# Norm roots as one power on GpSimd, earlier key masks, the last projection and norm by halves of tokens, and a new order of work

## The chip, the cores and the metric

The kernel runs on one core of a Trainium2 chip. The metric is the time of one execution in device microseconds; lower is better. Engines are named as in the profile: PE is TensorE (PEld its weight loads), DVE VectorE, ACT ScalarE, POOL GpSimd, SP SyncE, which here only issues loads and stores.

## The reference: what is computed

Four attention layers are chained on x (4 batches of 256 tokens of width 256) with one context of the same shape, all in float32:

```
x = L0(x, ctx)   # twice: x += cross_attention(layer_norm(x), ctx), 16 heads of 128, one learned key and value;
                 # then x += gelu(layer_norm(x) @ W1) @ W2
x = L1(x, ctx)   # x += attention(layer_norm(x), ctx, key mask), 16 heads of 16; then x += MLP(layer_norm(x))
x = L2(ctx, x)   # queries from x, keys and values from ctx and x together (512), key mask;
                 # then x += MLP(rms_norm(attention + x))
x = L3(x, ctx)   # 32 query heads of 8, 8 key heads, additive mask; then layer_norm(attention + x) * gamma + beta
```

Layer norm subtracts the mean and multiplies by rsqrt(variance + eps); the RMS norm of L2 multiplies by rsqrt(mean square + eps).

## The kernel before, in words

All of x (tile X), the context's transpose (ctxT) and the weights of the layer at work stay in SBUF; 128 tokens stand on the 128 partitions, so that a batch is two token tiles. Products go through eight PSUM banks (tags pj, s, et, o), and VectorE or ScalarE copies each out.

The code writes no instructions directly. It makes a list of some 2,500 `Task`s (line 172): each has a batch, a shape on TensorE ("full" 128x128, "rows" 32 rows, "cols" 32 columns, or none), a cost, the tasks it comes after, the ring buffers it takes and gives back, and `Post`s (line 160), the work of other engines behind it with a cost for each engine that may do it. `plan` (line 1617) then walks the list in time, engine by engine, by those costs, picks at each step the task of the highest rank among those that can start soonest (rank is the longest way to the end, less a handicap by stage, batch and kind, `HANDICAPS`, line 1740), and the instructions are issued in that order. `tc.keep_in_program_order` pins it: every engine runs its queue in exactly the planned order. Line 132 (134 in the kernel after) is the helper that issues nearly everything, so the profile is read by tiles.

Stage 0 is layer 0's two attentions (over four groups of four heads, two pairs of batches), stage 1 its MLP, stages 2 and 3 attention and MLP of L1, 4 and 5 those of L2, 6 is L3 with its closing norm. From stage 1 on a batch is a unit of work, and the batches overlap.

What the change and the prediction touch:

- `norm` (line 244) makes three tasks: `stats` on VectorE (mean and variance of two token tiles, and variance + eps), `root` on ScalarE (Ln, then Exp with scale -0.5), `apply` on VectorE (one Newton step of four instructions on 128x2 values, and the scaling of both tiles). It runs 28 times: 8 in stage 0, 4 for each of the three MLPs, 4 in L1's attention, 4 in L3's `closing` (line 888).
- `Layer.fill` (line 337) runs on GpSimd when layer 0's buffers are freed: small per-layer constants, and for L1 and L2 the key mask, loaded by GpSimd with the keys on the partitions (`hraw`) and turned into `hide`.
- `attention` (line 367): its `masks` tasks load the same mask per batch along the free axis (`mraw`) and turn it into `hide_r`; `keys.plus` makes from it the term that VectorE adds to the keys. `values.fill` sets the constant columns of the value tiles.
- "rows" tasks (`scores`, `maxima`, `weights`): products over 32 rows, for two row groups each. Two tasks of different `pair` run side by side on all four row groups. `SOLO` is what the planner adds for one that runs alone.
- `ending` and `project` (lines 516 and 783): an attention's output is divided by its sums (`quotients`, tile xo), turned back, projected (tile oT, weight w3o in L3) and added to X.
- `seven` (line 1037) makes a 512-wide product from seven products of 256, with sums of weights and of context prepared by GpSimd (`sums`, `value_sums`, `differences`); its second product is added to a bank that VectorE or ScalarE must first have copied out (tile u).
- `plan`'s constants (line 1608): NEAR 0.06 and SLACK 0.2, SOLO 2.0, HELD 0.9 (how much of GpSimd's remaining work is added to some VectorE tasks).

Of the kernel before, what the change touches and what calls it, by code (L numbers as in the profile page):

```python
# [51 lines left out]
def kernel(ctx: ExitStack, tc: tile.TileContext, a: dict, out: bass.AP):  # L52
# [52 lines left out]


# [95 lines left out]
    QK, VV, EQ, OT, XO, M3, HIDES, PLUS = (Ring([]) for _ in range(8))  # L202
    PO = [Ring([None, None]) for _ in range(2)]
    SHIFTS = [Ring([]), Ring([])]
    v_holds, raws = {}, {}
# [29 lines left out]
    def plus_row_to(b, after, dst, name):  # L235


        def run(e):
            for i in range(2):
                ge.tensor_tensor(dst()[:, i, :], dst()[:, i, :], row(name), ALU.add)  # L240

        return Task(b, None, 0, None, after, posts=[Post(("POOL",), 1450, run)])

    def norm(b, after, src, eps, mean, st, take=()):


        def stats(e):
            all_ = sm.tile([P, 8], F32, tag="mv8", name="mv8", bufs=8)
            mv = st["mv"] = all_[:, 0:4].rearrange("p (i c) -> p i c", i=2)
            v = st["v"] = all_[:, 4:6]  # L250
            st["r"] = all_[:, 6:8]
# [10 lines left out]
            if mean:  # L262
                ve.tensor_scalar(v, mv[:, :, 1], eps, None, ALU.add)
            else:
                ve.tensor_scalar(v, mv[:, :, 1], 1.0 / D, eps, ALU.mult, ALU.add)

        def root(e):
            r = st["r"]
            se.activation(r, st["v"], AF.Ln)
            se.activation(r, r, AF.Exp, scale=-0.5)  # L270

        def apply(e):

            v, r, mv = st["v"], st["r"], st["mv"]
            h = sm.tile([P, 2], F32, tag="ih", name="ih", bufs=2)
            ve.tensor_tensor(h, v, r, ALU.mult)
            ve.tensor_tensor(h, h, r, ALU.mult)
            ve.tensor_scalar(h, h, -0.5, 1.5, ALU.mult, ALU.add)
            ve.tensor_tensor(r, r, h, ALU.mult)
            st["apply"](mv, r)  # L280
# [10 lines left out]
        t = Task(b, None, 0, None, after, takes=take, posts=[Post(("DVE",), 1150, stats, near=True)])  # L291
        t = Task(b, None, 0, None, [t], posts=[Post(("ACT",), 400, root, EXP)])
        return Task(b, None, 0, None, [t], posts=[Post(("DVE",), 1400, apply, near=True)])
# [32 lines left out]
    class Layer:  # L326
# [9 lines left out]

        def fill(self):
# [15 lines left out]
            if key != 3:  # L353
                for g in range(2):
                    ge.tensor_scalar(
                        self.bkx[:, :, g], bk, sel16[:, g : g + 1], rowof[:, SHIFT[g] : SHIFT[g] + 1],
                        ALU.mult, ALU.add,
                    )

                mask, dtype = self.given  # L360
                raw = late_tile([P, B * S // P], f"hraw{key}", dtype=dtype)
                with nc.allow_non_contiguous_dma(reason="a mask, once"):
                    ge.dma_start(raw, mask.rearrange("o (c p) -> p (o c)", p=P))
                self.hide = late_tile([P, B * S // P], f"hide{key}")
                ge.tensor_scalar(self.hide, raw, 0.0, HIDE, ALU.is_equal, ALU.mult)

    def attention(L, b, after, hTs, dst, dst_after, weights_at):
# [11 lines left out]
        if key == 3:  # L379
# [3 lines left out]
            masks = Task(b, None, 0, None, after, takes=[(M3, st, "m")], posts=[Post(("SP",), 100, fetch)], lag=4.0)  # L383
        else:
            def fetch(e):
                ge.dma_start(raws[key], L.given[0][:, b * S : (b + 1) * S].to_broadcast([P, S]))

            def hidden(e):
                ge.tensor_scalar(st["hide_r"][2], raws[key], 0.0, HIDE, ALU.is_equal, ALU.mult)

            t = Task(b, None, 0, None, after, takes=[(HIDES, st, "hide_r")], posts=[Post(("POOL",), 700, fetch)], lag=3.0)
            masks = Task(b, None, 0, None, [t], posts=[Post(("POOL",), 1000, hidden)])
# [19 lines left out]
        def keys(t, after, q, give):  # L412
# [16 lines left out]
            for g in range(2):  # L429
# [6 lines left out]
                def add(e, g=g):  # L436
# [5 lines left out]
                    Task(b, None, 0, None, [masks], takes=[(PLUS, pl, g)], posts=[Post(("POOL",), 560, plus)])  # L442
# [14 lines left out]
        def values(si, after, give):  # L457
# [28 lines left out]
            t = Task(b, None, 0, None, after, takes=[(VV, st, f"V{si}")], posts=[Post(("POOL",), 600, fill)])  # L486
# [17 lines left out]
        for t in range(2):  # L504
            tq = queries(t, after, qs[t])
# [3 lines left out]
        if key != 3:  # L509
            Task(b, None, 0, None, behind=with_mask, gives=[(HIDES, st, "hide_r")])  # L510
        vs = [values(si, after, []) for si in range(len(L.sources))]
# [58 lines left out]
        def unit8(t, q):  # L570
            u = {}
            S_tasks, V_tasks = [], []
            for j in range(4):
                turned, Ss = [], []
                grab = Task(
                    b, None, 0, None, S_tasks or ready[t] + [masks],
                    takes=[(EE, u, j)] + ([(PO[1], u, "pm"), (PS, u, "po")] if j == 0 else []),
                )
                for pair in range(2):
# [30 lines left out]
                    for i in range(2):  # L610
# [5 lines left out]
                        def turns(i=i, v=v):  # L616
                            for kc in range(2):
# [10 lines left out]
                                b, "full", 0.47, turns, [tx], takes=[(PS, v, ("t", i))],  # L628
# [32 lines left out]
        def unit16(t, q):  # L661
# [55 lines left out]
            for kc in range(NCK):  # L717
                Ws = []
                grab = Task(
                    b, None, 0, None, shifted,  # L720
# [60 lines left out]
        w = {}  # L781

# [105 lines left out]
    def closing(b, after):  # L888
        st = {"xn": None}

        def apply(mv, r):
            for i in range(2):
                y = Xb(b)[:, i, :]
                ve.scalar_tensor_tensor(y, y, mv[:, i, 0:1], row("L3_xattn_gamma"), ALU.subtract, ALU.mult)
                ve.scalar_tensor_tensor(y, y, r[:, i : i + 1], row("L3_xattn_beta"), ALU.mult, ALU.add)
                dma.dma_start(out_t[:, b, i, :], y)

        st["apply"] = apply
        norm(b, after, lambda: Xb(b), 1e-6, True, st)
# [14 lines left out]
    for g in range(4):  # L914
        nc.gpsimd.dma_start(
            rows[_CS_ROWS:, :].rearrange("t (k g d) -> t k g d", k=4, g=4)[:, :, g, :], bk3
        )

# [36 lines left out]
    def columns(i, after, lag):  # L955
# [20 lines left out]
        return t if i == 2 else Task(0, None, 0, None, [t], posts=[Post(("POOL",), 800, scaled)])  # L976
# [25 lines left out]
    def differences(b, after, block, T):  # L1002
# [10 lines left out]
        return Task(b, None, 0, None, after, posts=[Post(("DVE", "POOL"), {"DVE": 1320, "POOL": 2900}, run, near=True)])  # L1013
# [9 lines left out]
    def sums(b, after, behind, w, key):  # L1023
# [11 lines left out]
        return Task(b, None, 0, None, after, posts=[Post(("POOL",), 2900, run)], behind=behind)  # L1035
# [102 lines left out]
    def context_sums(b):  # L1138
# [12 lines left out]
        return Task(b, None, 0, None, [t_ctx[b]], posts=[Post(("DVE", "POOL"), {"DVE": 840, "POOL": 1600}, run, near=True)])  # L1151
# [3 lines left out]
    def value_sums(after, behind, w):  # L1155
# [12 lines left out]
        return Task(0, None, 0, None, after, posts=[Post(("POOL",), 2900, run)], behind=behind)  # L1168
# [4 lines left out]
    for li in range(2):  # L1173
# [35 lines left out]
        for hg in range(NG):  # L1209
# [31 lines left out]
            def run(e, w=w):  # L1241
# [4 lines left out]
                0, None, 0, None, [t_bv], posts=[Post(("DVE", "POOL"), {"DVE": 600, "POOL": 1270}, run, near=True)]  # L1246
            )
            of_w = []
            for bp in range(2):
# [12 lines left out]
                t_learned = Task(b0, None, 0, None, [grab, t_cols[li]], posts=[Post(("POOL",), 400, learned)])  # L1262
# [224 lines left out]
    def run(e):  # L1487
# [15 lines left out]
        (XO, 1, [P, 2, P], "xo"),  # L1503
        (M3, 2, [P, 2, S], "m3"),
        (HIDES, 1, [P, S], "hide_r"),
# [3 lines left out]
    def open_late(e):  # L1509
# [12 lines left out]
        raws[1] = late_tile([P, S], "mraw1", mybir.dt.uint8)  # L1522
        raws[2] = late_tile([P, S], "mraw2", mybir.dt.int32)
# [15 lines left out]
    opened.fills = [(r, len(r.tiles), len(r.tiles) + n) for r, n, _, _ in later] + [(r, 0, 2) for r in SHIFTS]  # L1539
# [10 lines left out]
    def run(e):  # L1550
# [9 lines left out]
        k: Task(0, None, 0, None, [opened, t_rows], posts=[Post(("POOL",), 3500, lambda e, k=k: layers[k].fill())], lag=2.0)  # L1560
# [13 lines left out]
    for b in range(B):  # L1574
# [8 lines left out]
        at1 = attention(layers[1], b, [tt, t_w1, t_L[1]], st, lambda b=b: (Xb(b), Xb(b)), [tp], [])  # L1583
# [7 lines left out]
            [(EE, s2, "fT")],  # L1591
# [8 lines left out]
        to = attention(layers[3], b, [tt, t_w3, t_L[3]], st, lambda b=b: (Xb(b), Xb(b)), [tp], [])  # L1600
        closing(b, [to])
# [6 lines left out]
    LATE, NEAR, SOLO, TABLE, SLACK, HELD = 0.2, 0.06, 2.0, 1.3, 0.2, 0.9  # L1608
# [8 lines left out]
    def plan(handicap):  # L1617

        clock = {"PE": 0.0, "DVE": 3.3, "ACT": 2.0, "POOL": 5.5, "SP": 3.8}
# [4 lines left out]
        by_batch, by_kind = handicap  # L1626
# [18 lines left out]
        def do(group, start):  # L1645
# [16 lines left out]
            for t, p in queue:  # L1662
                def ends(e):
# [4 lines left out]
                    return begin + more + p.ns[e]  # L1668
# [176 lines left out]
```

## Time and profile before

| | us |
|---|---|
| median of 3 runs (lowest, highest) | 1366.13 (1364.66, 1367.18) |
| the profiled execution | 1366.06 |
| its span, first to last instruction | 1364.3 |
| mean granted TensorE clock | 0.991 |
| busy: PE, DVE, ACT, POOL | 1314.1, 831.3, 705.0, 190.3 |

The profile's page gives busy times by engine, forty slices of the span with one digit of busy tenths each, the chain of work that ended last, and the costliest groups of instructions. A line of a timeline gives the start, the length and the engine of one run of equal instructions, out tile<-in tiles, shapes and count, and in brackets how long the engine was idle before it and what ended that. A line of the table of stretches gives the stretch, its length, the busy time of PE, PEld, DVE, ACT and POOL in it, the granted TensorE clock, the DMA share and GB/s. A float32 matmul leaves two records, a turn (transpose by the identity) one.

### The profile page before, as it was taken

What the parts mean: (1) busy time and instruction counts of PE and PEld (TensorE: products, weight loads), DVE (VectorE), ACT (ScalarE), POOL (GpSimd) and SP (SyncE); (2) the same over time, 40 slices, a digit from 0 to 9 for tenths busy, and PEclk for the clock granted to TensorE, in tenths of its full rate; (3) what the DMA queues carried; (4) which work ended last, traced back from release to release, by engine and by line L of the source; (5) the groups of instructions that cost most, each with busy time, mean ns of one, the idle gap of its engine ahead of it and who ended that gap; (6) DMA issues with size and microseconds to landing.
All of it is one profiled execution on the core that took longest, in us unless ns stands there. A gap on an engine that the chain in (4) does not pass through costs nothing. (4 is left out here: it accounts for less than half of the span.)

```text
span 1364.3 us, 22474 instructions
## 1 busy us (share of the span) xinstructions
PE 1314.1 (96%) x8523; PEld 1038.3 (76%) x8523; DVE 831.3 (61%) x2305; ACT 705.0 (52%) x1717; POOL 190.3 (14%) x324
## 2 busy tenths in 40 slices
PE   7899999999999999999999899999999999999996
PEld 4788878888888788788888776677666668767764
DVE  7738546465664764755563468655567442886795
ACT  3445345345353453445544345644463554898795
POOL 7402020001321200200001422011011001000000
PEclk9999999999999999999999999999999999999998
DMA  6010020200200102001011320000000000000000
GB/s 230 17 47 1 1 78 1 77 1 1 78 17 31 31 1 78 1 0 47 1 67 53 92 79 4 5 1 5 6 1 5 2 1 1 1 13 13 2 10 16
DMA packets 25628, 38.01 MB, mean 28 GB/s; under 512 B 2244, under 2 KB 16086, under 8 KB 25392
## 3 DMA queue, kind: packets, MB, share of 16 engines
q1 hardware_dynamic: 24640, 35.56, 7.8%
q0 software_dynamic: 608, 0.76, 0.5%
q8 instruction: 67, 1.10, 0.4%
q14 instruction: 41, 0.34, 0.1%
q10 hardware_dynamic: 272, 0.26, 0.1%
HBM read 35.52 MB, written 1.05 MB: 27 GB/s over the span
## 5 line engine op out<-in xcount | busy, mean ns | idle before, releaser
L132 ACT ACTIVATE eq<-eq,nm 128x256 f32<-128x256 f32 x256 | 106.1, 503 | 0.5 <-DVE nm L132 0.5
L132 POOL TENSOR_TENSOR X<-X,rowbc 128x256 f32<-128x256 f32 x56 | 41.5, 762 | 410.9 <-DVE e L132 144.6
L132 DVE TENSOR_SCALAR E<-E,rinv 128x257 f32<-128x257 f32 x256 | 91.0, 420 | 2.3
L132 PE MATMUL ps_et<-qk 32*128 32x256 f32 (+1 forms) x254 | 79.9, 480 | 0.8 <-DVE shift L132 0.8
L132 PE MATMUL ps_s<-qk 32*128 32x256 f32 (+1 forms) x274 | 74.0, 464 | 5.8 <-DVE qk L132 5.5
L132 PE MATMUL ps_o<-qk 32*128 32x256 f32 (+1 forms) x266 | 73.7, 462 | 0.3 <-DVE eq L132 0.3
L132 PE MATMUL ps_pj<-qk 32*128 32x256 f32 (+1 forms) x230 | 64.5, 456 | 0.0
L132 POOL COPY kT<-lks 128x4 f32<-128x4 f32 x32 | 5.8, 195 | 378.6 <-PE ps_s L132 168.9
L132 PE MATMUL ps_et<-eq,qk 32*128 32x256 f32 x212 | 48.9, 402 | 0.2 <-DVE shift L132 0.2
L132 PE MATMUL ps_s<-eq,qk 32*128 32x256 f32 x204 | 48.8, 402 | 0.0
L132 PE MATMUL ps_pj<-eq,qk 32*128 32x256 f32 x184 | 47.0, 403 | 0.3 <-DVE shift L132 0.3
L132 DVE TENSOR_REDUCE shift<-ps_et 128x1 f32<-128x512 f32 (+1 forms) x58 | 39.3, 685 | 11.0 <-PE ps_pj L132 4.7
L132 PEld LDWEIGHTS ps_s<-qk 32*128 32x128 f32 x274 | 35.3, 187 | 12.2 <-issue 8.8
L132 DVE TENSOR_TENSOR X<-ps_et,X 128x512 f32<-128x512 f32 (+1 forms) x16 | 10.5, 658 | 55.4 <-PE ps_et L132 55.4
L132 ACT ACTIVATE E<-ps_o,nm 128x257 f32<-128x257 f32 x63 | 30.0, 477 | 27.6 <-DVE nm L132 27.4
L132 ACT ACTIVATE E<-ps_pj,nm 128x257 f32<-128x257 f32 x66 | 31.2, 476 | 22.2 <-DVE nm L132 22.1
L132 PE MATMUL ps_o<-eq,qk 32*128 32x256 f32 x168 | 42.5, 402 | 0.0
L132 PEld LDWEIGHTS ps_et<-qk 32*128 32x128 f32 x254 | 36.1, 188 | 8.2 <-issue 3.0
L132 PE MATMUL ps_et<-wo,cT 128*128 128x256 f32 x176 | 39.6, 379 | 0.0
L132 PEld LDWEIGHTS ps_o<-qk 32*128 32x128 f32 x266 | 35.1, 188 | 5.9 <-issue 2.9
L132 PE MATMUL ps_et<-kT,qT 128*128 128x257 f32 x122 | 34.9, 385 | 4.6 <-POOL X L132 4.5
L132 PE MATMUL ps_s<-kT,qT 128*128 128x257 f32 x132 | 39.1, 382 | 0.0
(581 smaller groups left out, 3868.6 us busy)
## 6 DMA issues: line engine op xcount, KB each, us to landing
wk<-in_L_xattn_wk_dram SPq DMA_DIRECT2D x8, 512.0 KB, 5.8
wv<-in_L_xattn_wv_dram SPq DMA_DIRECT2D x8, 512.0 KB, 6.8
wq<-in_L_xattn_wq_dram SPq DMA_DIRECT2D x8, 512.0 KB, 7.7
wo<-in_L_xattn_wo_dram SPq DMA_DIRECT2D x8, 512.0 KB, 4.0
bvb<-in_bv_dram SPq DMA_DIRECT2D x8, 256.0 KB, 7.8
bvl<-in_cols_dram SPq DMA_DIRECT2D x8, 256.0 KB, 7.8
f<-in_L_xattn_w_fc_dram SPq DMA_DIRECT2D x2, 1024.0 KB, 5.7
f<-in_L_xattn_mlp_w_dram SPq DMA_DIRECT2D x2, 1024.0 KB, 5.3
```

Of the source, the lines that this page charges most:

```text
L132: return lambda *args, **more: tc.keep_in_program_order(f(*args, **more))
```

## The change

The root becomes two instructions on GpSimd: add eps, raise to -0.5 (`minus_half` is a constant tile). The Newton step goes. The masks `hraw` are loaded by GpSimd at the start, behind its first loads; `fill` only tests them. The `masks` tasks of the attentions come after the work before the norm (`before`) and not after the transposed input, and there are two `hide_r` tiles, into which L2's row mask is loaded directly. L3's projection is cut into a first part (the first 128 of the reduction, both token tiles) and two parts of the second 128, one for each token tile, each followed by its own addition and its own closing norm. There are two xo tiles. Several planner costs are new (mostly higher, GpSimd's above all), three constants of `plan` and a factor on all VectorE and ScalarE costs ("wide") are now the last entry of `HANDICAPS`, HELD is 1.0, and the table of handicaps is another one, so nearly all instructions stand in a new order.

```diff
+    minus_half = const.tile([P, 2], F32, tag="mh", name="mh")
+    nc.vector.memset(minus_half, -0.5)
...
-            if mean:
-                ve.tensor_scalar(v, mv[:, :, 1], eps, None, ALU.add)
-            else:
-                ve.tensor_scalar(v, mv[:, :, 1], 1.0 / D, eps, ALU.mult, ALU.add)
-
-        def root(e):
-            r = st["r"]
-            se.activation(r, st["v"], AF.Ln)
-            se.activation(r, r, AF.Exp, scale=-0.5)
+        def root(e):
+            v, r, var = st["v"], st["r"], st["mv"][:, :, 1]
+            if mean:
+                ge.tensor_scalar(v, var, eps, None, ALU.add)
+                ge.tensor_tensor(r, v, minus_half, ALU.pow)
+            else:
+                ge.tensor_scalar(v, var, 1.0 / D, eps, ALU.mult, ALU.add)
+                ge.tensor_tensor(r, v, minus_half, ALU.pow)
...
-            v, r, mv = st["v"], st["r"], st["mv"]
-            h = sm.tile([P, 2], F32, tag="ih", name="ih", bufs=2)
-            ve.tensor_tensor(h, v, r, ALU.mult)
-            ve.tensor_tensor(h, h, r, ALU.mult)
-            ve.tensor_scalar(h, h, -0.5, 1.5, ALU.mult, ALU.add)
-            ve.tensor_tensor(r, r, h, ALU.mult)
-            st["apply"](mv, r)
+            st["apply"](st["mv"], st["r"])
...
+        def load(self):
+            mask, dtype = self.given
+            self.raw = const.tile([P, B * S // P], dtype, tag=f"hraw{self.key}", name=f"hraw{self.key}")
+            with nc.allow_non_contiguous_dma(reason="a mask, once"):
+                nc.gpsimd.dma_start(self.raw, mask.rearrange("o (c p) -> p (o c)", p=P))
...
-                raw = late_tile([P, B * S // P], f"hraw{key}", dtype=dtype)
-                with nc.allow_non_contiguous_dma(reason="a mask, once"):
-                    ge.dma_start(raw, mask.rearrange("o (c p) -> p (o c)", p=P))
                 self.hide = late_tile([P, B * S // P], f"hide{key}")
-                ge.tensor_scalar(self.hide, raw, 0.0, HIDE, ALU.is_equal, ALU.mult)
+                ge.tensor_scalar(self.hide, self.raw, 0.0, HIDE, ALU.is_equal, ALU.mult)
...
-            t = Task(b, None, 0, None, after, takes=[(HIDES, st, "hide_r")], posts=[Post(("POOL",), 700, fetch)], lag=3.0)
-            masks = Task(b, None, 0, None, [t], posts=[Post(("POOL",), 1000, hidden)])
+            t = Task(
+                b, None, 0, None, before, takes=[(HIDES, st, "hide_r")] + raw, posts=[Post(("POOL",), 700, fetch)], lag=3.0
+            )
+            masks = Task(b, None, 0, None, [t], posts=[Post(("POOL",), 1150, hidden)], gives=raw)
...
+            def part(k, qts):
+                for qt in qts:
+                    pe(
+                        w["pt"][2][:, qt * D : (qt + 1) * D], st["oT"][2][:, k, qt * P : (qt + 1) * P], L.w[3][:, k, :],
+                        k == 0 and qt == 0, k == 1, skip_group_check=True,
+                    )
+
+            def half(e, qt):
+                base, to = dst()
+                ve.tensor_tensor(to[:, qt, :], w["pt"][2][:, qt * D : (qt + 1) * D], base[:, qt, :], ALU.add)
+
+            first = Task(
+                b, "full", 0.86, lambda: part(0, (0, 1)), ends[:1] + dst_after, takes=[(PS, w, "pt")]
+            )
+            parts = []
+            for qt in range(2):
+                parts.append(
+                    Task(
+                        b, "full", 0.43, lambda qt=qt: part(1, (qt,)), [first, ends[1]], behind=list(parts),
+                        posts=[Post(("DVE",), 340, lambda e, qt=qt: half(e, qt), gives=[(PS, w, "pt")] if qt else [])],
+                        gives=[(OT, st, "oT")] if qt else [],
+                    )
+                )
+            return parts
...
+    for k in (1, 2):
+        layers[k].load()
...
-        (XO, 1, [P, 2, P], "xo"),
+        (XO, 2, [P, 2, P], "xo"),
         (M3, 2, [P, 2, S], "m3"),
-        (HIDES, 1, [P, S], "hide_r"),
+        (HIDES, 2, [P, S], "hide_r"),
...
-    LATE, NEAR, SOLO, TABLE, SLACK, HELD = 0.2, 0.06, 2.0, 1.3, 0.2, 0.9
+    LATE, TABLE, HELD = 0.2, 1.3, 1.0
...
-                    return begin + more + p.ns[e]
+                    return begin + more + p.ns[e] * wide
...
+        (0.4, 0.24, 0.71, 1.08),
```

The last line holds near, slack, solo and wide. The closing norm (not shown) is the same three steps for one token tile at a time, with its store.

## The prediction

> **What bounds the kernel now.** I read the page first (busy shares, slices, chain), then the table of stretches, then the waits of TensorE alone by stretch, then the timelines of the stretches where it waits. The page gives the bound:
>
> ```profile
> PE 1314.1 (96%) x8523; PEld 1038.3 (76%) x8523; DVE 831.3 (61%) x2305; ACT 705.0 (52%) x1717; POOL 190.3 (14%) x324
> ...
> POOL 7402020001321200200001422011011001000000
> ```
>
> TensorE is busy for 1314.1 of 1364.3 us, so work taken off another engine pays only where TensorE waits for it: 50.2 us in all. GpSimd stands at 14%, but its slices say where it is full: at the opening (7, 4) and around slice 23. The table of stretches (stretch, length, then busy time by engine) splits the 50.2:
>
> ```profile
> 0.00:50.00 50.00, 37.23 (x123) 23.64 (x124) 37.13 (x89) 16.11 (x41) 32.97 (x59) 0.93 0.47 158
> 50.00:700.00 650.00, 638.58 (x3152) 553.52 (x3151) 386.45 (x903) 300.31 (x853) 77.15 (x128) 0.99 0.09 30
> 700.00:800.00 100.00, 94.41 (x512) 81.38 (x511) 45.40 (x129) 38.68 (x87) 21.68 (x52) 0.98 0.21 63
> 800.00:1300.00 500.00, 493.23 (x4249) 346.02 (x4248) 313.75 (x972) 303.81 (x628) 58.51 (x87) 1.00 0.03 7
> 1300.00:1364.30 64.30, 50.62 (x495) 33.77 (x492) 48.54 (x214) 46.08 (x111) 0.00 (x0) 0.94 0.04 14
> ```
>
> TensorE idles 12.8 us in the opening, 11.4 in layer 0, 5.6 at the change of layers, 6.8 in layers 1 to 3, 13.7 at the end. The single waits that make these up, from the waits and the timelines (start, length, then idle time and its releaser in brackets):
>
> ```profile
> 39.05 1.20 PE L132 MATMUL ps_et<-kT,qT 128*128 128x257 f32 x2 [4.54 <-POOL X L132]
> ```
> ```profile
> 202.01 1.54 PE L132 MATMUL ps_o<-HT,f 128*128 128x256 f32 x4 [3.01 <-DVE u L132]
> ```
> ```profile
> 756.09 0.26 POOL L132 TENSOR_SCALAR hide<-hraw 128x8 f32<-128x8 uint8 x1 [7.83 <-DMA hraw<-in_mask_dram]
> ...
> 763.49 0.26 POOL L132 TENSOR_SCALAR hide<-hraw 128x8 f32<-128x8 int32 x1 [4.33 <-DMA hraw<-in_mask_dram]
> ```
> ```profile
> 776.35 0.80 PE L132 MATMUL ps_s<-qk 32*128 32x256 f32 x2 [5.49 <-DVE qk L132]
> ```
>
> At 39.05 the X sum of GpSimd is only the latest event. VectorE is the cause: it hasn't been idle since 7.0 us and finishes the qT that this matmul reads at 38.91. At 202.01 (and 556.79, alike) VectorE is late too: its four quotients on E take 3.2 us since GpSimd runs sums beside them (0.82 us each beside GpSimd's sums, 0.35 alone, from the single records). At 756 and 763 GpSimd stands still for two mask loads; what is queued behind them (row sums 766.64 to 770.8, the row mask's load, its fill, the key terms to 777.4) makes TensorE wait at 776.35.
>
> **The change, part by part.** The sum is made against the profiled execution's 1366.06 us (span 1364.3 and 1.8 around it), which lies within the three runs (1364.66 to 1367.18, median 1366.13).
>
> Counted from the two orders of instructions: TensorE has 4953 matmuls and turns in both. VectorE goes from 2307 to 2173 instructions: 28 times five small ones go (0.19 for the epsilon, 0.19, 0.16, 0.21, 0.18 for the Newton step, 0.93 us a norm, 26 us in all). ScalarE loses 56 roots of 0.20 and 4 of 18 table loads of 1.28, 16 us. GpSimd gains 64 small ones (an epsilon and a power for each of 24 norms and 8 half norms). None of it is TensorE's own time, so only the stretches count.
>
> *Opening: -5.0 (ends 0 and -6.9).* In front of the qT at 38.9, VectorE's order loses four epsilons (0.17, 0.17, 0.17, 0.40), four Newton steps (1.78, 1.72, 0.78 and 1.67, stretched by GpSimd's sums), the second bvb difference (0.60, now GpSimd's) and the fourth batch's two normalised tiles (1.43, now behind it): 8.9 us from an engine that was never free. TensorE can win what it idles behind VectorE: 4.54 at 39.05 and 2.3 at three waits for xn (17.75, 20.10, 20.90); the rest (4.64 and 1.2) are first loads that nothing changes. Against it: the roots now stand in GpSimd's queue, the first behind four sums of 0.73 that start when ctxT is there (7.4), so not before 10.4; VectorE's first statistics end about then (7.4 + 0.2 + 1.6 + 1.2). The two mask loads cost GpSimd 1.0 each at 5.7, where it was idle for 1.84; 0.2 shows. Their 5 KB join loads at a DMA share of 0.93, behind wk and x, ahead of nothing that TensorE asks for before 23. I take -5.0, nearer the far end since VectorE's sum is larger than the gap.
>
> *The power itself.* No row shows one. Below stands the 128x16 difference (0.23), above the 256-wide mask test (1.08). With its epsilon (0.2 to 0.3) a root is 0.5 to 1.4; it replaces 0.44 on ScalarE and 0.75 on VectorE with one hop fewer. I take 0.6, near the small row, and count the middle of the program at nothing.
>
> *Layer 0: -8 (ends 0 and -14).* The order is new, so I asked what makes a wait: a task placed too near behind the one that it waits for. Walking both orders at 0.43 us a 128x256 matmul and 0.1 to 0.2 a change of tile shape, and taking off the copies between at 0.3 to 0.6, 166 of layer 0's 744 TensorE tasks had under 1 us to spare before and 73 have now; with less than nothing, 23 and 1. The idle time is 11.4, and each wait costs more than its idle time: the turns at 198.07 would have been followed at 198.5, the next matmul came at 202.01, 3.5 for 3.01. So some 14 are there, and 56% of the tight places go: -8.
>
> *Change of layers: -5.0 (ends -3 and -5.5).* The two waits (7.83, 4.33) and issues (1.01, 0.97) leave GpSimd's order here, 14.1 us. In the new order the row masks no longer wait for the layer's transposed input. 5.49 goes; 0.5 is kept for three norm roots (0.6 each) that now stand in this queue ahead of the key terms. SP's order puts layer 2's four weights ahead of the MLP's two (1 MB more, landing 12.0 after their issue at worst now); the MLP asks for them some 20 us later, so nothing.
>
> *Layers 1 to 3: -1 (ends +4 and -5).* By the same walk 72 tight tasks become 62: 14% of 6.8.
>
> *Row-group pairs: +7.0 (ends +3.5 and +7.0).* The order before runs the score products of 32 rows always as two tasks side by side on the four row groups, 128 times. The new one has 120 pairs and 16 tasks alone (planned with the price of a lone one cut from 2.0 to 0.71). A pair takes 0.87 because its records in one row group follow each other at 0.21 (1293.52, 1293.74, 1293.95); a lone task has the same four. So 8 x 0.87 more, unless the second half fills time that was idle anyway.
>
> *Changes of shape: -1.4.* 311 become 298, at 0.11 (a first record 0.32 before the next, not 0.21).
>
> *End: -2.2 (ends -1.2 and -3.9).* From 1352.75, where the last turns end, to the end are 11.55: projection 3.40, add 0.75, statistics 1.4, roots 0.5, Newton 0.75, scale and shift 1.85, the store's 2.9. By halves: the first token half is projected at 0.43 x 6 = 2.55, its add and statistics end at 3.7, its root at 4.5; the second half's root at 5.3, its scale and shift, behind the first half's, at 6.4, the store's 2.9: 9.3. The projection's eight records stand 0.43 apart here, twice the 0.21 of elsewhere, at a granted clock of 0.50 (stretch 1354 to 1356.2); I keep 0.43, since the waits for the quotients ahead of them stay, and at 0.21 they would save 1.7 more, the far end. The Trainium skill (TensorE: Matmul & The Clock Gate, "Part 1: The HAM clock gate") says that TensorE falls to half clock after an idle window of about 3.4 us and needs as long a busy one to return; the trace agrees with the half, though the waits ahead of it here are of 0.6 to 1.2 each. By that rule the sum stays as it is; were a busy stretch enough to keep the clock, it would be 1349.
>
> Sum: -5.0 - 8 - 5.0 - 1 + 7.0 - 1.4 - 2.2 = -15.6, so 1350.5, put as **1350**.
>
> **The rivals.**
> *Waits go nearly everywhere (0.16).* All far ends: -6.9 - 14 - 5.5 - 5 + 7 - 1.4 - 3.9 = -29.7, 1336. For it: one tight place below zero in layer 0. Against: VectorE and ScalarE are full as well from 1290 on (9.96 of 10 us for ScalarE at 1330 to 1340).
> *Waits only move (0.17).* Spare time by count is not the late queue itself. Then layer 0 and layers 1 to 3 give nothing, the opening 3, the rest as above: -3 - 5 + 7 - 1.4 - 2.2 = -4.6, 1361.
> *GpSimd's queue becomes the norm's wait: slower (0.14).* Each root stands in order behind sums of four (2.9 us) or a mask load (up to 3.0 between issue and test). If half of the 32 roots show 2.0 each to TensorE, 32 us come on top: 1382. It decides from 15.6 / 32 = 0.5 us shown a root. For it: seven roots stand right behind such groups. Against: GpSimd's share is 14%, and batches are interleaved, so TensorE has other work.
> *A power's code is fetched at its first use (0.03).* GpSimd's first sum (0.45) and first scalar (0.31) were no longer than the next, and the longest unexplained gap is 0.4; so by rows 1351. The Trainium skill (GPSIMD Engine Reference, "2.1 Instruction dispatch") gives some 6 us for the first call of a freshly loaded kernel; in the opening that would make about 1356 by its figure.
> That the change does not do what it says is excluded by the order: 32 powers on GpSimd, no Newton step left.
>
> **How the numbers follow.** 0.50 for the forecast (1342 to 1358). A measurement here can tell about 0.2%, 2.7 us, so "same" is 1363.4 to 1368.8. Faster: 0.50 + 0.16 + 0.03 + 0.12 of "only move" = 0.81; same 0.06; slower 0.13. The range 1334 to 1364 reaches both neighbours and leaves out the slow rival and the edges.
>
> **What would show it.** Opening: first kT,qT matmul before 36. Layer 0 (50 to 700): TensorE idle under 6, no wait of 3.0 on u. Layers' change: no wait on hraw, first qk products with no idle over 1. Lone tasks: TensorE's busy time some 7 longer in layers 1 to 3. End: 9 to 10 us behind the last turns. Wrong if TensorE waits for tiles behind a GpSimd root, or if new waits of over 2 us stand in layer 0.

## The result, and the profile after

The changed kernel takes **1351.53 us** (median of 4, 1349.59 to 1353.99), beside 1365.93 us of the kernel before on the same chip (4 runs): a ratio of 0.9896, 95% interval 0.9876 to 0.9915. That is 14 us less; the prediction was 1350. Run again later it gave 1351.24 us, ratio 0.9890 (0.9877 to 0.9904). The profiled execution is the one of 1349.59 us (span 1347.8), 16.5 less than the profiled one before.

The page after, engine shares and GpSimd's slices:

```profile
PE 1313.6 (97%) x8523; PEld 1050.7 (78%) x8523; DVE 813.5 (60%) x2171; ACT 691.3 (51%) x1659; POOL 218.4 (16%) x385
...
POOL 9420010200142002000015231030010020110000
```

TensorE is busy for the same time as before (1314.1); what went is idle time, 50.2 to 34.2 us. The table of stretches after (stretch, length, busy by engine, granted clock, DMA share, GB/s) says where:

```profile
0.00:50.00 50.00, 42.75 (x174) 30.51 (x175) 39.06 (x96) 22.20 (x62) 45.14 (x77) 1.00 0.51 167
50.00:700.00 650.00, 646.86 (x3239) 567.05 (x3238) 393.18 (x895) 299.54 (x842) 76.99 (x131) 1.00 0.09 29
700.00:800.00 100.00, 97.71 (x623) 80.78 (x622) 43.57 (x107) 35.13 (x69) 38.32 (x80) 1.00 0.24 77
800.00:1300.00 500.00, 487.38 (x4117) 346.16 (x4116) 303.00 (x924) 298.66 (x603) 54.74 (x90) 0.99 0.02 4
1300.00:1347.80 47.80, 38.88 (x379) 26.21 (x376) 34.72 (x152) 35.80 (x84) 3.18 (x8) 0.95 0.04 13
```

TensorE's idle time, before and after: opening 12.8 and 7.3, layer 0 11.4 and 3.1, change of layers 5.6 and 2.3, layers 1 to 3 6.8 and 12.6, end 13.7 and 8.9. Four stretches gave time back and one took some. (From 700 on the same stretch doesn't hold quite the same work in both: from 800 to the last turns, where the work ends alike, the idle time is 12.3 and 14.7.)

The single waits after, as the timelines have them. The opening: the first kT,qT product stands at 28.66 (before 39.05), with one short wait ahead of it.

```profile
27.73 1.10 PE L134 MATMUL ps_pj<-craw,f 128*128 128x256 f32 x4 [0.72 <-DVE u L134]
...
28.66 0.60 PE L134 MATMUL ps_s<-kT,qT 128*128 128x257 f32 x2
```

The change of layers: no wait on hraw is left, but a root stands behind the fills in GpSimd's queue. Its statistics were done at 712.49; the root starts at 718.30, VectorE waits 4.70 for it, and TensorE 2.29 for VectorE.

```profile
712.31 0.18 DVE L134 BATCH_NORM_AGGREGATE mv<-st 128x2 f32<-128x6 f32 x1
...
717.11 1.10 POOL L134 TENSOR_SCALAR bqx<-cols,selq 128x2 f32<-128x2 f32 x4
718.30 0.22 POOL L134 TENSOR_SCALAR mv<-mv 128x2 f32<-128x2 f32 x1
718.61 0.72 POOL L134 TENSOR_TENSOR mv<-mv,mh 128x2 f32<-128x2 f32 x1
...
719.36 0.73 DVE L134 TENSOR_SCALAR e<-X,mv 128x256 f32<-128x256 f32 x2 [4.70 <-POOL mv L134]
...
719.88 0.82 PE L134 MATMUL ps_et<-ident,e 128*128 128x128 f32 x4 [2.29 <-issue]
```

TensorE's row says only "issue": it is the e of VectorE, one step up the chain, that is late. Layer 3's projection by halves has a wait that the prediction did not foresee, here at 1191.53, and alike at 1250.65 (2.62):

```profile
1188.21 0.70 PE L134 MATMUL ps_pj<-w3o,oT 128*128 128x256 f32 x2
...
1191.06 0.42 DVE L134 TENSOR_TENSOR X<-ps_pj,X 128x256 f32<-128x256 f32 x1
...
1191.53 0.70 PE L134 MATMUL ps_pj<-w3o,oT 128*128 128x256 f32 x2 [2.62 <-DVE X L134]
```

The first two records of TensorE are the first half of the tokens, the next two the second half. Both halves lie in one PSUM bank, and the second waits until VectorE has added the first to X. That add takes 0.42 of the wait; for most of the rest VectorE works off eight instructions on another tile (eq, 0.42 each, from 1188.30) that stand ahead of the add in its queue. The end shows it too, with 0.52:

```profile
1338.82 1.46 PE L134 MATMUL ps_o<-w3o,oT 128*128 128x256 f32 x6
...
1340.32 0.42 DVE L134 TENSOR_TENSOR X<-ps_o,X 128x256 f32<-128x256 f32 x1 [1.72 <-PE ps_o L134]
...
1340.79 0.70 PE L134 MATMUL ps_o<-w3o,oT 128*128 128x256 f32 x2 [0.52 <-DVE X L134]
1341.53 0.42 DVE L134 TENSOR_TENSOR X<-ps_o,X 128x256 f32<-128x256 f32 x1 [0.79 <-PE ps_o L134]
```

The halves follow each other instead of overlapping. But the projection's records stand 0.22 apart here, not 0.43: the clock held.

### The profile page after: what moved, and what is told of

Read it like the earlier page. It is cut to its first block, busy times and chain, and to the rows that moved or that the text cites. A ratio compares the mean times of both kernels' runs of the same rounds, so it can differ in the third digit from the quotient of the medians.

```text
span 1347.8 us, 22397 instructions
## 1 busy us (share of the span) xinstructions
PE 1313.6 (97%) x8523; PEld 1050.7 (78%) x8523; DVE 813.5 (60%) x2171; ACT 691.3 (51%) x1659; POOL 218.4 (16%) x385
## 4 chain that ended last, share of the span: by engine, by line
PE 90%; DVE 7%; ACT 2%; issue 1%; DMA 1%; POOL 0%; SPq 0%; DVEq 0%; ACTq 0%
PE ps_o L134 23%; PE ps_pj L134 23%; PE ps_s L134 23%; PE ps_et L134 21%; DVE E L134 2%; DVE eq L134 1%; ACT eq L134 1%; DVE shift L134 1%; DMA wk<-in_L_xattn_wk_dram 1%; ACT qk L134 0%; DVE qk L134 0%; DVE X L134 0%; DVE e L134 0%; DVE craw L134 0%; DVE xo L134 0%
## 5 line engine op out<-in xcount | busy, mean ns | idle before, releaser
L134 DVE TENSOR_SCALAR E<-E,rinv 128x257 f32<-128x257 f32 x256 | 97.9, 445 | 2.3
L134 PE MATMUL ps_s<-qk 32*128 32x256 f32 (+1 forms) x270 | 85.2, 476 | 0.0
L134 POOL TENSOR_SCALAR mv<-mv 128x2 f32<-128x2 f32 (+1 forms) x32 | 7.4, 233 | 454.9 <-DVE mv L134 454.4
L134 PE MATMUL ps_pj<-qk 32*128 32x256 f32 (+1 forms) x242 | 75.2, 470 | 0.0
L134 PE MATMUL ps_pj<-eq,qk 32*128 32x256 f32 x224 | 55.2, 405 | 0.0
L134 DVE TENSOR_REDUCE shift<-ps_s 128x1 f32<-128x512 f32 (+1 forms) x54 | 36.5, 683 | 20.9 <-PE ps_o L134 11.3
L134 POOL TENSOR_SCALAR plus<-hide_r,rowof,bkx 128x256 f32<-128x256 f32 x32 | 17.7, 559 | 146.6 <-DVE qk L134 146.2
L134 DVE TENSOR_TENSOR X<-ps_o,X 128x256 f32<-128x256 f32 (+1 forms) x20 | 10.4, 518 | 51.2 <-PE ps_o L134 51.2
L134 DVE TENSOR_TENSOR X<-ps_pj,X 128x512 f32<-128x512 f32 (+1 forms) x18 | 10.3, 573 | 50.1 <-PE ps_pj L134 50.1
L134 DVE TENSOR_REDUCE shift<-ps_o 128x1 f32<-128x512 f32 (+1 forms) x47 | 31.8, 683 | 13.6 <-PE ps_et L134 5.4
```

What stands on the lines that cost most here:

```text
L134: return lambda *args, **more: tc.keep_in_program_order(f(*args, **more))
```

## The experiments

Each was timed in five rounds against the kernel before on the same chip. Unless said otherwise each keeps the planner's order and changes only what is issued.

**The change's parts alone, in the order of before.** `before_masks` issues the two mask loads with the opening's:

```
-                    ge.dma_start(raw, mask.rearrange("o (c p) -> p (o c)", p=P))
...
+    for k in (1, 2):
+        layers[k].load()
```

> The kernel before with one edit: the two mask loads (hraw) are issued with the opening's loads, the order of all else kept. The theory of the prediction (the two GpSimd waits of 7.83 and 4.33 us at 756 and 763 are what delays the key terms, and so the first qk products): 1361 us, 3 to 5.5 less than before, and the 5.49 us wait of TensorE at 776 is gone. Rival (the products wait for something else that is nearly as late, the key terms' own chain or the row mask): 0 to 1 us less, a wait of 4 or more stays at the same matmul.

Measured 1361.78 us (before 1366.15), ratio 0.9963 (0.9951 to 0.9976): 4.4 less, and the wait of 5.49 at the first qk products is 0.51:

```profile
772.69 0.48 PE L132 MATMUL ps_s<-qk 32*128 32x256 f32 x2 [0.51 <-DVE qk L132]
```

The theory holds. `before_roots` moves epsilon and root to GpSimd, and takes Newton's step out, in the place of the old root:

```
-                ve.tensor_scalar(v, mv[:, :, 1], eps, None, ALU.add)
+                ge.tensor_scalar(v, var, eps, None, ALU.add)
...
-            se.activation(r, st["v"], AF.Ln)
-            se.activation(r, r, AF.Exp, scale=-0.5)
+            ge.tensor_tensor(r, v, minus_half, ALU.pow)
...
```

> The kernel before with one edit: epsilon and root as two GpSimd instructions in the place where ScalarE's Ln and Exp stood in the order, Newton's step and epsilon gone from VectorE; the order of all else kept, table loads kept. The theory of the prediction (what the lighter VectorE gives is the opening's queue behind qT, and the middle gives nothing): 1361 to 1363 us, about 3 to 5 less, all of it before 50 us and at the end. Rival 1 (VectorE's 26 us less empty its queue everywhere): about 1355, with the waits on u at 202 and 557 shorter. Rival 2 (in an order that did not plan for it, roots stand behind GpSimd's sums and mask loads): 1370 or more, with TensorE waiting for tiles behind a GpSimd root.

Measured 1361.33 us (1356.55 to 1364.22), ratio 0.9959 (0.9944 to 0.9974): 4.8 less. The theory's total came out, but as the sum of a larger gain and a loss that rival 2 had named. The stretches of this kernel (in its slowest execution, 1364.22, which is the profiled one):

```profile
0.00:50.00 50.00, 43.09 (x164) 29.91 (x165) 35.20 (x85) 18.51 (x48) 42.67 (x75) 1.00 0.49 168
700.00:800.00 100.00, 87.40 (x463) 74.22 (x462) 37.57 (x93) 32.39 (x68) 25.94 (x61) 0.93 0.21 60
```

The opening idles 6.9 instead of 12.8, at a clock of 1.00 instead of 0.93; this edit alone makes the whole gain of the change's opening. The change of layers idles 12.6 instead of 5.6, since two roots stand behind the mask loads and the work queued behind these (GpSimd's order and TensorE's wait, from the timeline):

```profile
748.31 0.26 POOL L135 TENSOR_SCALAR hide<-hraw 128x8 f32<-128x8 uint8 x1 [8.09 <-DMA hraw<-in_mask_dram]
...
760.47 0.72 POOL L135 TENSOR_TENSOR mv<-mv,mh 128x2 f32<-128x2 f32 x1
...
761.86 1.08 PE L135 MATMUL ps_et<-ident,eq 128*128 128x128 f32 x4 [12.05 <-issue]
```

`before_both` has both edits.

> The kernel before with both edits, masks early and roots on GpSimd, order kept. If the parts add up as the theory has it: about 1357, 9 less than before, and the other 5 of the change's 14 belong to the new order (with its halves and rings). Rival (the new order gives nothing of its own, the gain is the two edits): about 1352. Rival (each edit's gain needs the new order): 1363 or more.

Measured 1357.39 us, ratio 0.9939 (0.9925 to 0.9953): 8.8 less, nearly the sum of the two (9.2); the wait of 12.05 is 6.29, now behind the copy of Wk, which waits for its load. The other 5.6 of the change's 14.4 are what the rest of the change does in sum (order, halves, tiles), for and against.

**Layer 0's waits: amount or order?** `before_quotients_later` moves one task in VectorE's queue, at two places:

```
+    for at in (376, 1050):
+        steps.insert(at + 4, steps.pop(at))
```

> The kernel before with one edit of the order: in layer 0 the second group of four quotients on VectorE (3.1 us beside GpSimd's sums) is moved behind the two row minima, u and the q sum that stood behind it, at the two places whose TensorE waits on u are 3.01 us each (202.01 and 556.79); TensorE's, ScalarE's and GpSimd's orders are unchanged, and no work is taken away. Theory (layer 0's waits come from the place of a task in VectorE's queue, not from how much VectorE has to do, so an order alone takes them away, as the new order did): both waits go, 5 to 6 us less than before, about 1360.5. Rival (VectorE is simply late there, and the quotients come to be what TensorE waits for): no less than 1 us is gained, and a wait on E or eT of some 3 us stands in the place of each.

Measured 1360.71 us (before 1366.58), ratio 0.9960 (0.9947 to 0.9974): 5.9 less with no work removed. At the first place (before: 3.01 on u at 202.01):

```profile
200.25 0.55 PE L132 MATMUL ps_pj<-ident,E 128*128 128x128 f32 x3 [1.71 <-DVE E L132]
200.63 1.03 PE L132 MATMUL ps_o<-HT,f 128*128 128x256 f32 x4
```

The waits on u are gone; a wait of 1.7 on E stands in the place of each, where the rival said 3. So 1.3 of idle time is saved at each. The rest of the 5.9 is the clock's: behind the waits of 3.01 TensorE was granted 0.57 from 202 to 206, and 0.69 and 0.88 from 556 to 564, which by its busy time loses 1.7 and 1.5; behind those of 1.7 it was granted 1.00. So the order alone is worth this much, with the same amount of work. It does not take all of the wait: the 1.7 that stays at each place is a wait for the quotients, which is what the rival said, at about half its size.

**What a lone row-group task costs.** `after_lanes_alone` issues the two tasks of every pair one after the other:

```
-            while lanes:
-                for lane in list(lanes):
-                    if next(lane, lane) is lane:
-                        lanes.remove(lane)
+            for lane in lanes:
+                for _ in lane:
+                    pass
```

> The changed kernel with one edit: in every one of its 120 pairs of row-group tasks the products of the two tasks are issued one task after the other, and not in turn; same products, same order of all else. Theory of the prediction (a task alone takes as long as a pair, 0.87 us, since its four records follow each other at 0.21): about 0.87 us more for each pair, 104 in all if TensorE's time is what counts there, 1440 to 1455. Rival (the two tasks' records overlap across row groups even when they are issued one after the other, or a task alone costs TensorE only half of a pair): 1351 to 1375, and then the price of 7 us for the 16 lone tasks of the change was too high.

Measured 1351.01 us, ratio 0.9888 (0.9874 to 0.9901): no difference from 1351.24, and none of the theory's 104 us. The order of issue inside a pair costs nothing: in this trace a pair issued so still takes 1.08 (860.75 to 861.83), since the records of its two tasks overlap anyway. It says nothing on a task with other work behind it, so the conclusion that I had written beside the rival was too wide. `before_pairs_apart` settles that: at 24 places the next full-array task is issued between the two of a pair.

```
...
+            for _ in group[0].run():
+                pass
+            between[0].run()
+            for _ in group[1].run():
+                pass
...
```

> The kernel before with one edit of TensorE's order: at 24 places where a pair of row-group tasks stands ahead of a full-array task that needs neither of them, that full task is issued between the two, so that each of the two runs alone; same work, and the orders of VectorE, ScalarE and GpSimd are unchanged. Theory of the prediction (a task alone costs as much as a pair, 0.87 us, and each place adds two changes of shape of 0.11): 18 to 27 us more than before, 1384 to 1393. Rival (a task alone costs half of a pair): 3 to 8 us more, 1369 to 1374.

Measured 1399.29 us, ratio 1.0250 (1.0233 to 1.0267): 33 more, 1.37 a place, above the theory's range. From this kernel's timeline, two lone tasks with their eight records each:

```profile
804.41 1.13 PE L132 MATMUL ps_s<-eq,qk 32*128 32x256 f32 x8
805.48 0.66 PE L132 MATMUL ps_et<-ident,eq 128*128 128x128 f32 x4
806.06 1.13 PE L132 MATMUL ps_pj<-eq,qk 32*128 32x256 f32 x8
807.12 1.07 PE L132 MATMUL ps_et<-e,V 128*32 128x256 f32 x16
```

From start to next start a lone task holds TensorE for 1.06 to 1.07; a pair, 16 records, for 1.08. Summed from the trace (start to next start, idle time taken off), the 32-row products hold TensorE for 149.5 us in the kernel before, 173.5 in this one, 162.2 in the changed kernel, with the same records in all three. So these products cost 12.7 more in the changed kernel; part of that is half clock (below).

**The wait on X.** `after_parts_ahead` issues both halves of the second k part ahead of both adds:

```
-                        b, "full", 0.43, lambda qt=qt: part(1, (qt,)), [first, ends[1]], behind=list(parts),
+                        b, "full", 0.43, lambda qt=qt: None if qt else part(1, (0, 1)), [first, ends[1]], behind=list(parts),
```

> The changed kernel with one edit in the order kept: in layer 3's projection the second half of the second k part is issued with the first half, ahead of both adds (the later task emits nothing), so that no matmul writes to the bank while VectorE's add of the first half reads it. Theory (TensorE's four waits for X, 2.62 at 1191, 2.62 at 1251, 0.63 and 0.52 at the end, are made by the split, since the two halves share a bank): 4 to 6 us less than the changed kernel, about 1346, no wait on X at ps_pj, ps_et and ps_o in layer 3. Rival (VectorE is late there anyway, and the matmuls behind wait for its next results instead): within 1.5 us of the changed kernel.

Measured 1342.77 us, ratio 0.9826 (0.9811 to 0.9842); the changed kernel's control is `after_again`, 1351.24.

> The changed kernel unchanged, as the control for the others of this call: 1350 to 1353 us, as in its first runs (median 1351.5).

The waits on X are gone; the projection runs on with both halves, and the two adds follow later:

```profile
1189.88 1.13 PE L134 MATMUL ps_pj<-w3o,oT 128*128 128x256 f32 x4
...
1192.72 0.75 DVE L134 TENSOR_TENSOR X<-ps_pj,X 128x256 f32<-128x256 f32 x2
```

The gain is 8.5 by the medians, above the 4 to 6 expected and above the 6.4 that the four waits add up to. The clock is the likely rest: its mean is 0.995 over the four executions of this kernel and 0.992 over the eight of the changed kernel, some 3 us. How it comes about, the two profiled executions of the changed kernel show. In the first, behind the wait of 2.62 (stretches of 2 us):

```profile
1192.00:1194.00 2.00, 2.00 (x11) 1.75 (x10) 0.42 (x1) 2.00 (x7) 0.00 (x0) 1.00 0.00 0
1194.00:1196.00 2.00, 2.00 (x13) 1.76 (x12) 0.18 (x1) 0.80 (x2) 0.00 (x0) 1.00 0.00 0
```

In `after_again`, behind the same wait of the same length:

```profile
1192.00:1194.00 2.00, 2.00 (x5) 1.64 (x6) 0.42 (x1) 2.00 (x6) 0.00 (x0) 0.50 0.00 0
1194.00:1196.00 2.00, 2.00 (x6) 1.55 (x6) 0.00 (x0) 1.11 (x3) 0.00 (x0) 0.50 0.00 0
```

The granted clock falls to half in one and not in the other (the eighth number of a line), for 6.8 us, some 3 us lost on top. Behind the second such wait it is the other way round: the clock falls for 3.4 us behind 1250.65 in the first and holds behind 1253.94 in `after_again`. So a wait of this length costs between 2.6 and 5.6. Over all of TensorE's records the half clock takes 6.8 us in the first execution and 9.8 in `after_again`, which is most of the 3.3 by which their spans differ. The Trainium skill (PSUM — Partial Sum Buffer, "Terms") says that TensorE and another engine must not touch the same bank and quadrant at once; the trace agrees in that the second half, which writes other columns of the bank, waits for the reader of the first. That wait is for a semaphore of the program, so no run here shows what the chip would do without it.

**The root in GpSimd's queue.** `after_fills_later` emits the fills of layers 2 and 3 with Wk's head-wise copy:

```
+        layers[2].fill()
+        layers[3].fill()
         w3 = layers[3].w
...
+        k: Task(0, None, 0, None, [opened, t_rows], posts=[Post(("POOL",), 2100, lambda e, k=k: layers[k].fill() if k == 1 else None)])
```

> The changed kernel with one edit: GpSimd's fills of layers 2 and 3 (selq, bqx, bkx, hide, 3.5 us), which stand ahead of a norm's root at 718.3 in its queue, are emitted with the head-wise copy of Wk instead, some 6 us later; TensorE's order is kept. Theory (TensorE's 2.29 us at 719.88 is a wait for a tile whose root stands in GpSimd's queue from 712.5 to 718.3): 2 to 2.3 us less than the changed kernel, the wait at ps_et<-ident,e gone. Rival (the fills' new place delays the key terms by as much, or VectorE's other work holds the tile): within 1 us of the changed kernel.

Measured 1348.26 us, ratio 0.9868 (0.9855 to 0.9882): 3.0 less than the control, more than the 2 to 2.3 expected. The wait was the queue; the same turns now stand without one:

```profile
718.55 0.60 PE L134 MATMUL ps_et<-ident,e 128*128 128x128 f32 x4
```

`after_two_powers` doubles every power:

```
                 ge.tensor_tensor(r, v, minus_half, ALU.pow)
+                ge.tensor_tensor(r, v, minus_half, ALU.pow)
...
```

> The changed kernel with every power issued twice (the second writes the same root again), which puts 0.72 us (0.57 for the half norms) more behind each of the 32 statistics, 22 us more on GpSimd. Theory (a root on GpSimd is hidden beside other batches' work in most places, and shown in the opening, at 719.88 and at the end only): 1 to 3 us more than the changed kernel, 1352.5 to 1354.5. Rival (the root stands on TensorE's way wherever a norm is): 8 us or more on top, 1360 or more.

Measured 1356.82 us, ratio 0.9926 (0.9914 to 0.9939): 5.6 more than the control, between the theory's 1 to 3 and the rival's 8. Of some 22 us more on GpSimd a quarter shows, 0.17 a root: mostly hidden, but less well than I thought. The wait at 719.88 has grown from 2.29 to 3.05; where the rest shows isn't settled, since waits that lower the clock differ between single executions.

**Together.** `after_ahead_fills` has both of the mended places.

> The changed kernel with both edits of the earlier runs, the second k part of layer 3's projection ahead of both adds and the fills of layers 2 and 3 behind the norms' roots. If the two gains (8.8 and 3.0 by their medians against the changed kernel) are separate, as theirs are different waits in different stages: 1339 to 1342 us, faster than both kernels. Rival (what waits behind one comes to be shown by the other): 1343 or more.

Measured 1340.21 us (1336.51 to 1342.76), ratio 0.9802 (0.9785 to 0.9819): 11.0 less than the control, the two gains nearly added. It beats both kernels.

One thing was left: in all seven profiles of the new order up to here the clock falls for 7 to 10 us from about 810 on, with no wait over 0.5 us ahead of it. The stretches of this kernel there:

```profile
806.00:810.00 4.00, 3.35 (x17) 2.11 (x19) 4.00 (x9) 0.00 (x0) 0.77 (x2) 0.95 0.00 0
810.00:814.00 4.00, 4.00 (x23) 2.67 (x23) 3.98 (x9) 1.02 (x2) 2.08 (x3) 0.50 0.12 24
814.00:818.00 4.00, 4.00 (x34) 3.44 (x30) 2.65 (x4) 1.27 (x2) 2.19 (x3) 0.50 0.06 13
```

TensorE is recorded as busy for 3.35 of the first 4 us and all the time behind them, but much of it with lone row-group tasks, which use half of the array's rows. `after_full_between` adds full-array products there, whose result is overwritten:

```
+        if group[0].shape == "rows" and len(group) == 1 and (group[0].stage, group[0].b) == (2, 1) and "maxima" in group[0].kind:
+            bank_ = next(h[k][2] for r, h, k, i in taken if r is PS)
+            for _ in range(2):
+                pe(bank_[:, :S], ident, rowbc[:, :S], True, True)
```

> The kernel of the last combination (parts ahead, fills later) with idle work added: two 128x256 products on the full array (0.43 us each at full clock), whose result is overwritten, ahead of each of the four lone maxima tasks of batch 1 in layer 1 (around 807 to 816), 3.4 us in all. In every run of the new order so far TensorE's granted clock falls to 0.5 from 810 to some 820, with no wait over 0.5 us ahead of it, in this stretch of lone row-group tasks. Theory (row-group tasks that fill half of the array or less count to the clock as idling does): with full-array work between them the granted clock stays at or near 1.00 in 806 to 824, and the time is 1 to 3 us less than the 1340.2 of the combination in spite of the added work. Rival (the clock falls there for another reason): the clock is 0.5 in that stretch as before, and the time is 3 to 7 us more.

Measured 1338.56 us (1338.04 to 1340.2; before 1366.73), ratio 0.9796 (0.9782 to 0.9809). The same stretches:

```profile
806.00:810.00 4.00, 4.00 (x28) 2.76 (x24) 4.00 (x8) 0.00 (x0) 0.50 (x2) 1.00 0.00 0
810.00:814.00 4.00, 3.74 (x32) 2.31 (x30) 3.57 (x9) 1.13 (x3) 1.96 (x3) 1.00 0.18 30
814.00:818.00 4.00, 3.86 (x33) 2.66 (x32) 2.84 (x5) 1.86 (x4) 2.19 (x3) 1.00 0.03 7
```

The clock holds at 1.00. Useless work of 3.4 us costs nothing at the least; the 1.6 us by which this is faster than the kernel without it lies within the intervals, so the time alone does not show a gain. The edit did more than add full-array work: the waits of 0.46 and 0.16 that stand at 806.42 and 808.81 without it are gone too, and the lone task at 806.42 takes 1.13 (there at 807.75) instead of 1.72, so some waiting may lie inside what was recorded as busy. Idle time alone does not make this fall, though. In `after_fills_later` TensorE idles 0.23 from 806.4 to 809.8, and the clock falls right behind it; in the changed kernel's first profile it idles 1.93 from 1189.6 to 1193.0, and the clock holds.

## Why the prediction was right, and where its steps were wrong

Direction and size came out, 1350 against 1351.5, and the sum of the steps, -15.6, against -16.5 between the two profiled executions. Not all the steps did.

- **Opening, -5.0**: the mechanism holds, and `before_roots` shows that moving the root and taking out Newton's step does it alone. Idle time fell by 5.5; with it the clock of the stretch rose from 0.93 to 1.00, some 3.2 us more (the kernel before works 6.5 us of its opening at half clock). Mis-sized: the half clock behind the waits was not in the term.
- **The power, 0.6**: measured 0.95 (0.23 and 0.72; 0.57 for the half norms). Taking the middle at nothing was right within a few us, by `after_two_powers`. The first power takes 0.73, like the others, so no code was fetched that the trace could show.
- **Layer 0, -8**: idle time fell by 8.3, and there is no wait on u; with the half clock behind the two waits (1.7 and 1.5) it is 11.5. That a wait comes from a task's place in a queue is shown at two places by `before_quotients_later`; that the count of tight places sizes the sum is one agreement, not a proof. The price "3.5 for 3.01" was too low, as in the opening.
- **Change of layers, -5.0**: the masks are worth 4.4 alone, near the 5.0 taken. But "0.5 is kept for three norm roots" failed: 2.29 of idle time stands behind one root, 3.0 with what follows. This is the third rival, GpSimd's queue, and the prediction's own sign of being wrong, true at one place (and at 12.05 in the order of before). It did not decide: its time was 1382, and even a doubled power shows 0.17 a root, not 0.5.
- **Layers 1 to 3, -1**: wrong. Idle time rose by 5.8 in 800 to 1300, and by 2.4 from 800 to the last turns. The step looked at tasks placed too near each other and not at the bank that the split's two halves share, 2.62 twice here and 0.63 and 0.52 at the end, 6.4 in all. No rival had it, though the diff shows it: one `pt`, an add of its first half, and a matmul into its second half behind that add.
- **Row-group pairs, +7.0**: the mechanism holds, a lone task costs a pair's time. Mis-sized: 12.7. Eight more such times at 1.06 are 8.5. Of the other 4.2 the half clock explains 2.3: it takes 3.8 from such products in the changed kernel, around 810 to 820, but took 1.5 in the kernel before too, behind its wait at 776.35. The last 1.9 stay open.
- **Changes of shape, -1.4**: not measured apart.
- **End, -2.2**: from the last turns to the end 8.8 after 11.55, -2.7, but not by an overlap of the halves' products and adds, which follow each other. The projection's records stand 0.22 apart, where I kept 0.43 "since the waits for the quotients ahead of them stay". They shrank: 0.34 and 0.65 ahead, for 0.64, 0.76 and 1.16. On the clock the far end was the right one, though two of the six profiles with the old waits hold the clock there as well.

So the direction and the main mechanisms were right, and that the total came out to within 2 us was luck: the steps that were too small (opening, layer 0, end) and the costs left out or too low (the shared bank, the root behind the fills, the dear lone tasks) nearly cancel, and one gain has no step at all. TensorE's records, from start to next start with idle time taken off, hold it for 1313.4 us before and 1313.2 after. The row-group products take 12.7 more of this, so all others take 12.9 less. About 5 of these are half clock that went away; the other 8 stand in no step but the 1.4 for changes of shape, and no run shows where they lie.

## What to carry to other kernels

Price a wait of TensorE with the clock behind it: from a trace, take the start-to-start loss and not the idle time alone. When a task is split so that its parts can overlap, issue all writes to a shared bank ahead of the first read (a bank for each part was not run). When work moves to an engine with room on the whole, look at its queue at the places where it is full; a move that pays in one stage can wait behind a load in another.

## What the runs showed of the hardware

- The granted clock falls to 0.5 behind a single wait of 2.62 in one execution and not in another; behind three waits of 0.64, 0.76 and 1.16 within 5 us at the end it fell in four of the six profiles that have them; behind 0.34 and 0.65 it held in all eight. The Trainium skill (TensorE: Matmul & The Clock Gate, "Part 1: The HAM clock gate") gives an idle window of about 3.4 us; the trace shows falls behind less idle time in one piece than that.
- While TensorE works, the half clock lasts 3.41 us or a whole multiple (6.83, 10.24, 13.65) in every trace, and its starts lie on a grid: those at 810.74 and 1251.06 in the changed kernel's first profile are 129 steps of 3.413 apart. The wait of 2.62 ahead of 1250.65, behind which the clock fell, lies inside one step; the one ahead of 1253.94 in `after_again`, behind which it held, is cut in 1.2 and 1.4. That the place on the grid decides is not shown, since the wait near 1191 is cut in 0.7 and 1.9 in the one and in 1.9 and 0.8 in the other, and the clock fell only in the second.
- The clock also falls to 0.5 behind a stretch of lone row-group products with little idle time (0.23 to 0.68 us in the 3.4 us ahead of the fall, in seven profiles), and with four times two full-array products between them it stays at 1.00. How much of this is the kind of product and how much the short waits that went with the edit is open.
- The order in which the two tasks of a pair are issued doesn't matter (1351.01 for 1351.24); whether a full-array task stands between them does (1.37 us a place).
